# Moving the distances ahead of the update, and conv1 one place away from the first turn of x, in a 64-graph GNN kernel

## The chip, the cores and the metric

The kernel runs on one core of one Trainium2 chip. The metric is the device time of one execution in microseconds (us). Single executions of one kernel scatter by some us out of 2250 here, so differences of a few us are read from five rounds with a 95% interval, and from where instructions start in the traces.

## The reference

64 graphs of 256 nodes with 256 features pass two layers. Cut to what matters:

```python
# layer 0
xc = x^T;  h = relu(bn(conv1d(xc, conv1_w, 0)))           # conv1: one tap
h  = bn(conv1d(h, conv2_w, 8));  x_conv = relu(h + xc)^T   # conv2: 17 taps
s  = x @ w_se.T + b_se
A  = exp(-(|s_n|^2 + |s_m|^2 - 2 s_n.s_m)) * adj           # "distances", exp, mask
x_nmp = A @ relu(x @ w_msg.T + b_msg)                      # "messages", "passing"
r, z  = sigmoid(gates of [x_conv, x_nmp] and x)            # rz
n     = tanh(gi_n + r * gh_n)                              # the update's tanh
x = layernorm(x + (1-z)*n + z*x)                           # x1; h is its normalized form
# layer 1
h = layernorm(x)
x = layernorm(x + relu(adj @ h @ W_rel + b_rel + h @ W_root))   # project, aggregate, y
```

## The kernel before

The 64 graphs go through in 8 batches of 8. While the graphs of one batch pass through both layers, conv1 and conv2 of the next batch are dealt out between their steps. conv2 is turned into 16 small products per feature block ("filter products", `ps_k`), with trees of sums on VectorE around them. The order on every engine is the order in which the program issues; I call it the engine's queue. The trace shows it on ScalarE: in batch 1 the exp started at 288.72, behind a tanh that started at 288.19, though its distances were done near 287. `bank(...)` hands out one of the eight PSUM tiles of one pool (`bufs=8`), to which the matmuls here write; a new product on such a bank comes after the reading of the older one, and this shows as waits: in the profile of before the filter products stood 11.6 us, over 14 places, for the exp that reads the distances.

Two things make up the stream. The generator `conv(b)` hands out the convolution; each `yield None` ends a place:

```python
def conv(b):
    ...
    for g in range(0, BG, 2):                        # four pairs of graphs
        for c in range(C):                           # "turn" of x on TensorE
            ps = bank("ps_xTc")
            for j in range(4):
                nc.tensor.transpose(ps[:, j*P:(j+1)*P], xn[:, j, c*P:(c+1)*P], ident)
            nc.scalar.copy(xTc[:, c, :], ps)                          # L458
        nc.scalar.dma_start(out=xt_dram[pair], in_=xTc)
        fetch(g + 4)
        yield PE_WEIGHT
        yield None
        pss = []
        ...                                          # conv1: ps_c <- w1, xTc (L466), relu (L482)
    yield None
    if b > 0:
        yield from fold(0, BG)                       # DVE, 128x2048 each (L432)
    ...

def products(b, first, sums):                        # one triple of filter products
    p1, p2, p3 = bank("ps_k1"), bank("ps_k2"), bank("ps_k3")
    ...
    def take():
        nc.scalar.copy(k1, p1)                                        # L400
        nc.vector.tensor_sub(..., k1, p3)                             # L401
        nc.vector.tensor_add(..., k1, p2)                             # L402
    return take
```

The loop over the graphs interleaves it, one `pump()` at a time. `step(up)` runs the next part of the update, `step(y_left)` the last part of the graph before:

```python
def distances(k):                                    # ps_dist (L685), exp (L687)
    pss = [bank("ps_dist") for _ in range(C)]
    for m in range(C):
        nc.tensor.matmul(pss[m][:, :N], lr[r, 0, m*P:(m+1)*P], lr[r, 1, :], ...)
    for m in range(C):
        nc.scalar.activation(AT[k][:, m, :], pss[m][:, :N], AF.Exp, bias=ns[:, m:m+1], scale=2.0)

def update(k):
    stt(nn, ...); stt(nn, ...)                       # DVE (L104)
    nc.scalar.activation(nn, nn, AF.Tanh)            # L833
    yield                                            # first step ends
    nc.vector.tensor_sub(w, XG[k], nn)               # L837, then two more on w, then stats
    ...                                              # q, sh on GpSimd (L846 to L851)
    yield                                            # second step ends
    ...                                              # h on DVE (L856), x1 on ScalarE (L859)
    yield

def aggregate(k):
    ...                                              # ps_out, y on DVE, q and sh on GpSimd
    yield
    for n in range(C):
        nc.scalar.activation(y[:, n, :], ...)                         # L910
    nc.scalar.dma_start(out=out[k]..., in_=y)                         # L911
    yield

for k in ...:                                        # the graphs of batches 0 to 6
    up = update(k)
    gates_rz(k, 0);   pump()
    gates_n(k, 0);    step(y_left);   pump()
    transposes_h(k - 1);              pump()
    gates_rz(k, 1);   pump()
    passing(k + 1);   pump()
    factors(k + 2);   gates_n(k, 1);  pump()
    project(k - 1)
    step(up);         pump()
    distances(k + 2)
    step(up);         pump()
    messages(k + 3)
    step(up);         pump()
    mask(k + 2)
    agg = aggregate(k - 1); step(agg); step(agg); pump()
    y_left = agg
```

The last batch has a loop of its own, without convolution, in which VectorE makes sums for a cheaper form of the gates (`ps_a`, `ps_d`, ...; L786, L791).

## Time and profile before

| | before |
|---|---|
| time, median of 3 runs (range) | 2256.24 us (2254.48 to 2259.09) |
| TensorE (PE) busy | 2210.0 of 2252.8 us, 98% |
| VectorE (DVE) / ScalarE (ACT) / GpSimd (POOL) busy | 76% / 34% / 21% |
| PE's largest waits | exp of the distances (L687) 11.6 us; copy of turned x (L458) 7.1; filter take (L401) 4.7 |

PE is the bound, and nothing in the change shortens its work. So only its waits are of interest: who released it, how long, and what it ran into next. The lines themselves stand in the prediction.

### The profile page before, as it was taken

To read this page: it belongs to the slowest core of one execution; us is meant where nothing else is said; L and a number is where in the kernel's file an instruction comes from. 1 tells how busy PE (TensorE), PEld (TensorE's weight loads), DVE (VectorE), ACT (ScalarE), POOL (GpSimd) and SP (SyncE) were. 2 spreads that over 40 slices of the span, in tenths; PEclk is the share of its full clock that TensorE was granted. 3 is DMA by queue.
4 is the path that set the end of the run, shared out by engine and by line. 5 is a ranking of instruction groups with operands and counts; after the bars stand their busy time and mean duration, and the time that the engine had idled before them with its cause. 6 is when DMAs were issued, how large, how long until landed. Compare 5 with 4: busy or idle time off the path is not lost.

```text
span 2252.8 us, 24641 instructions
## 1 busy us (share of the span) xinstructions
PE 2210.0 (98%) x8400; PEld 1465.9 (65%) x8400; DVE 1721.0 (76%) x3329; ACT 767.1 (34%) x1587; POOL 469.8 (21%) x933
## 2 busy tenths in 40 slices
PE   8999999999999999999999999999999999999998
PEld 5775666666666666656766566665666666666665
DVE  6976889478892988749987498965979478896675
ACT  6433223432235322443224432244222432224333
POOL 0101212221221221203212221221212222212212
PEclk9999999999999999999999999999999999999999
DMA  5931432314423143232522334222432314321110
GB/s 148 317 111 60 143 108 84 103 52 140 135 76 103 38 151 120 75 107 67 167 72 76 102 114 142 76 87 74 131 122 75 113 52 140 114 85 50 42 33 20
DMA packets 212682, 226.69 MB, mean 101 GB/s; under 512 B 22103, under 2 KB 203854, under 8 KB 212558
## 3 DMA queue, kind: packets, MB, share of 16 engines
q1 hardware_dynamic: 190128, 191.27, 26.8%
q10 hardware_dynamic: 22430, 33.86, 4.3%
q8 instruction: 67, 1.10, 0.2%
q14 instruction: 57, 0.47, 0.1%
HBM read 179.22 MB, written 45.88 MB: 100 GB/s over the span
## 4 chain that ended last, share of the span: by engine, by line
PE 80%; DVE 15%; issue 2%; POOL 1%; ACT 1%; DMA 1%; ACTq 0%; SPq 0%; POOLq 0%; DVEq 0%
PE ps_rz L715 15%; PE ps_k L385 11%; PE ps_rz L713 8%; PE ps_n L727 7%; PE ps_out L882 7%; PE ps_c L466 5%; DVE XF L104 5%; PE ps_nmp L697 5%; PE ps_msg L647 4%; PE ps_out L894 4%; PE ps_n L725 4%; PE ps_w L230 2%; DVE w L104 2%; DVE bst L824 1%; PE ps_dist L685 1%
## 5 line engine op out<-in xcount | busy, mean ns | idle before, releaser
L104 DVE SCALAR_TENSOR_TENSOR XF<-XF 128x512 f32<-128x512 f32 (+2 forms) x800 | 507.8, 665 | 7.4
L846 POOL TENSOR_SCALAR q<-mv 128x2 f32<-128x2 f32 x63 | 31.9, 506 | 1442.1 <-DVE mv L825 1442.1
L385 PE MATMUL ps_k<-w,XF 128*128 128x256 f32 x1316 | 300.1, 384 | 12.9 <-ACT AT L687 11.6
L385 PEld LDWEIGHTS ps_k<-w,XF 128*128 128x128 f32 x1316 | 248.0, 191 | 59.8 <-ACT AT L687 17.3
L728 DVE TENSOR_TENSOR gn<-ps_n,brzn 128x512 f32<-128x512 f32 x114 | 78.4, 688 | 198.1 <-PE ps_n L727 198.1
L719 ACT ACTIVATE rz<-rz 128x512 f32<-128x512 f32 x114 | 71.8, 630 | 463.5 <-DVE rz L718 463.5
L882 PE MATMUL ps_out<-wrr,hT 128*128 128x512 f32 x504 | 226.6, 592 | 0.0
L713 PE MATMUL ps_rz<-whh,xT 128*128 128x512 f32 x456 | 215.6, 595 | 0.0
L715 PE MATMUL ps_rz<-wih,xc 128*128 128x512 f32 x456 | 214.3, 592 | 0.0
L715 PE MATMUL ps_rz<-wih,nmp 128*128 128x512 f32 x456 | 214.3, 592 | 0.0
L718 DVE TENSOR_TENSOR rz<-ps_rz,brzn 128x512 f32<-128x512 f32 x114 | 77.7, 682 | 152.9 <-PE ps_rz L715 152.9
L882 PEld LDWEIGHTS ps_out<-wrr,hT 128*128 128x128 f32 x504 | 95.9, 190 | 96.1 <-issue 84.6
L715 PEld LDWEIGHTS ps_rz<-wih,xc 128*128 128x128 f32 x456 | 86.7, 190 | 109.0 <-issue 108.8
L715 PEld LDWEIGHTS ps_rz<-wih,nmp 128*128 128x128 f32 x456 | 86.7, 190 | 109.0 <-issue 109.0
L658 ACT ACTIVATE msg<-msg 128x512 f32<-128x512 f32 x61 | 38.4, 630 | 339.2 <-DVE msg L656 339.2
L647 PE MATMUL ps_msg<-wms,xT 128*128 128x260 f32 x512 | 131.8, 395 | 4.7 <-DVE XF L401 4.7
L362 DVE TENSOR_TENSOR XF<-XF 128x512 f32<-128x512 f32 (+3 forms) x128 | 126.2, 1011 | 1.7
L466 PE MATMUL ps_c<-xTc,w 128*128 128x512 f32 x256 | 116.1, 596 | 7.1 <-ACT xTc L458 7.1
L697 PE MATMUL ps_nmp<-AT,msg 128*128 128x256 f32 x512 | 121.1, 379 | 0.0
L713 PEld LDWEIGHTS ps_rz<-whh,xT 128*128 128x128 f32 x456 | 82.8, 192 | 58.2 <-issue 55.0
L894 PE MATMUL ps_out<-hr,adj 128*128 128x256 f32 x504 | 119.6, 380 | 0.0
L883 ACT COPY hr<-ps_out 128x256 f32<-128x256 f32 x126 | 46.8, 372 | 213.8 <-PE ps_out L882 213.8
(197 smaller groups left out, 3790.2 us busy)
## 6 DMA issues: line engine op xcount, KB each, us to landing
w<-w2m SPq DMA_DIRECT2D x105, 768.0 KB, 5.9
xn<-in_x_dram SPq DMA_DIRECT2D x32, 512.0 KB, 4.4
xt<-xTc ACTq DMA_DIRECT2D x32, 512.0 KB, 3.3
xT<-xt SPq DMA_DIRECT2D x64, 256.0 KB, 3.0
xb<-in_x_dram SPq DMA_DIRECT2D x32, 512.0 KB, 5.9
adj<-in_adjT_dram SPq DMA_DIRECT2D x64, 256.0 KB, 2.8
x<-in_x_dram SPq DMA_DIRECT2D x64, 256.0 KB, 3.0
out_dram<-y ACTq DMA_DIRECT2D x63, 256.0 KB, 2.2
```

Source lines behind the costliest of these rows:

```text
L104: nc.vector.scalar_tensor_tensor(o, in0, s, in1, op0=op0, op1=op1)
L362: (nc.vector.tensor_add if add else nc.vector.tensor_sub)(sl(o, n), sl(a, n), sl(b, n))
L385: nc.tensor.matmul(ps, X[:, slot, c * P:(c + 1) * P], w(m, c), start=(c == 0), stop=(c == C - 1))
L466: nc.tensor.matmul(pss[o], w1[:, c, o * P:(o + 1) * P], xTc[:, c, :], start=(c == 0), stop=(c == C - 1))
L647: nc.tensor.matmul(ps[:, :D + 4], XT[k][:, c, m * P:(m + 1) * P], wms[:, c, :], start=(c == 0), stop=(c == C - 1 and not idle))
L697: nc.tensor.matmul(ps[:, d * N:(d + 1) * N], MSG[k][:, m, d * P:(d + 1) * P], AT[k][:, m, :], start=(m == 0), stop=(m == C - 1))
L713: nc.tensor.matmul(prz, XT[k][:, c, q], whh[:, c, 0:2 * D], start=(c == 0), stop=False)
L715: nc.tensor.matmul(prz, t, wih[:, i, 0:2 * D], start=False, stop=(i == 3))
L725: nc.tensor.matmul(pn[:, D:], XT[k][:, c, q], whh[:, c, 2 * D:], start=(c == 0), stop=(c == C - 1))
L727: nc.tensor.matmul(pn[:, :D], t, wih[:, i, 2 * D:], start=(i == 0), stop=(i == 3))
L882: nc.tensor.matmul(ps, hT[:, c, n * P:(n + 1) * P], wrr[:, c, :], start=(c == 0), stop=(c == C - 1))
L894: nc.tensor.matmul(po, ADJ[k][:, m, n * P:(n + 1) * P], hr[:, m, :], start=False, stop=(m == C - 1), skip_group_check=True)
```

## The change

Its intent is to remove the two largest waits of PE: the copy of turned x gets more time before conv1 reads it, and the exp of the distances no longer queues on ScalarE behind a tanh that is waiting for VectorE. The diff in full:

```diff
@@ conv(b) @@
             fetch(g + 4)
             yield PE_WEIGHT
             yield None
+            if b > 0 and g == 0:
+                yield None
             pss = []
@@ the loop over the graphs @@
             if k > 0:
                 project(k - 1)
+            if k + 2 < B:
+                distances(k + 2)
             step(up)
             pump()
-            if k + 2 < B:
-                distances(k + 2)
             step(up)
             pump()
@@ the loop of the last batch @@
         project(k - 1)
-        step(up)
         if k + 2 < B:
             distances(k + 2)
+        step(up)
         step(up)
```

I call the three hunks part 1 (place of conv1), part 2 (exp first, in the loop) and part 3 (exp first, in the last batch).

## The prediction

> **What bounds the kernel now.** I read first the busy shares of the page, then the waits of PE, then the timeline at the places where PE waits. The busy shares:
>
> ```profile
> span 2252.8 us, 24641 instructions
> ...
> PE 2210.0 (98%) x8400; PEld 1465.9 (65%) x8400; DVE 1721.0 (76%) x3329; ACT 767.1 (34%) x1587; POOL 469.8 (21%) x933
> ```
>
> The change alters no matmul, so only the 42.8 us that PE isn't busy can be won; some 8 us of them are start and end. The view of waits for PE names the rest:
>
> ```profile
> PE ps_k L385 <- ACT AT L687: 11.6, 14, 1.1
> PE ps_c L466 <- ACT xTc L458: 7.1, 10, 1.8
> PE ps_msg L647 <- DVE XF L401: 4.7, 13, 0.5
> PE ps_xc L574 <- DVE XF L104: 3.4, 1, 3.4
> PE ps_hT L869 <- DVE h L856: 2.6, 1, 2.6
> ...
> PE ps_a L786 <- DVE XF L791: 0.9, 1, 0.9
> ```
>
> (columns: total us, times, longest.) The change aims at the first two: the exp (L687) frees the PSUM bank that a product of the filters (ps_k) takes over, and the copy of the turned x (L458) is what conv1 (ps_c) reads. So the ceiling is about 19 us, 0.8%. But a wait counts only if PE isn't held a moment later by somebody else. The timeline (start, duration) at a wait of the first kind, from batch 1:
>
> ```profile
> 283.02 0.69 DVE L728 TENSOR_TENSOR gn<-ps_n,brzn 128x512 f32<-128x512 f32 x1 [4.17 <-PE ps_n L727]
> ...
> 286.35 0.70 PE L685 MATMUL ps_dist<-lr 4*128 4x256 f32 x4
> ...
> 288.19 0.63 ACT L833 ACTIVATE nn<-nn 128x512 f32<-128x512 f32 x1 [1.36 <-DVE nn L104]
> 288.72 0.82 ACT L687 ACTIVATE AT<-ps_dist,ns 128x256 f32<-128x256 f32 x2
> 289.23 4.58 PE L385 MATMUL ps_k<-w,XF 128*128 128x256 f32 x20 [1.12 <-ACT AT L687]
> ...
> 294.17 0.68 DVE L401 TENSOR_TENSOR XF<-XF,ps_k 128x512 f32<-128x512 f32 x1
> ...
> 294.91 1.14 PE L647 MATMUL ps_msg<-wms,xT 128*128 128x260 f32 x4 [0.22 <-DVE XF L401]
> ```
>
> The distances are ready at about 287, but the exp queues behind the tanh, which waits for DVE until 288.19. That is the wait meant. Yet 5.7 us later PE stands again, for L401 on DVE. From gn at 283.02 to L401 I followed every row of DVE: each starts where the one before ends, with no idle time. The start at 283.02 was set by PE before either wait.
>
> At a conv1, and in the last batch:
>
> ```profile
> 434.30 0.60 PE L869 MATMUL ps_hT<-ident,h 128*128 128x128 f32 x4
> 434.90 1.07 ACT L458 COPY xTc<-ps_xTc 128x512 f32<-128x512 f32 x2 [0.58 <-PE ps_hT L869]
> 435.54 3.70 PE L466 MATMUL ps_c<-xTc,w 128*128 128x512 f32 x8 [0.64 <-ACT xTc L458]
> ...
> 2154.94 0.53 DVE L791 TENSOR_TENSOR XF<-ps_a,brzn 128x384 f32<-128x384 f32 x1
> ...
> 2156.20 1.89 PE L786 MATMUL ps_a<-wsum,XF 128*128 128x256 f32 x6
> ```
>
> Only four small transposes lie between the turn of x and conv1. In the last batch PE writes onto the bank of ps_a 0.73 us after DVE has read it: little slack.
>
> [...]
> - [...] the exp ran 288.72, behind a tanh that came late, though its input was done near 287.
> - [...] So a tile takes the bank of an earlier one, and the order in which banks come free decides. The waits on L687 and L401 agree: both name readers of older tiles.
> - [...] swapping them reloads nothing. The trace agrees: one table load, 1283 ns, in the whole run.
> - [...] So I measure PE's losses from start to start.
>
> **Part 1, conv1 one place later (7 batches).** The order of instructions on PE changes here alone: the gates rz of the second half (12 records, 5.1 us) move between the first turn and conv1, and each later turn and conv1 slides by one, the last conv1 landing behind the distances. The copies need 1.07 us plus a hop, so the wait goes. Its size, start to start: from ps_hT at 434.30 to the next turn at 439.07 are 4.77 us; four transposes cost 0.43 and eight records of conv1 3.43 elsewhere, so 0.9 us are lost. Six batches look so: 6 x 0.9 = 5.4 us. The later conv1s get the neighbours that the next one has now (nmp, then sT and n), which show no wait; the last gets ps_out and dist, 4 us.
>
> Side effect on DVE: the folds now come after the update's w. In the first batch, graph 0, DVE stands 1.89 us before the folds, then w follows, and PE waits 2.64 us for h (transposes at 204.03). Now w fills that idle stretch. By hand: distances near 187.6, exp until 189.3, tanh until 189.9, w 190-193.2, folds (6.6 us) until 199.8, message sums until 200.8, h until 201.5. PE is ready near 200.7, so the transposes start near 201.5: 2.5 us won, with the 0.5 us of its conv1 inside. In the six other batches h is done near 474.6 against PE near 476: no wait either way.
> Part 1: 5.4 + 2.5 = 7.9 us.
>
> **Part 2, distances ahead of the update, in the filter products.** PE's order doesn't change, only ScalarE's: exp, exp, tanh. The exps end near 287.8, the bank is free when PE wants it (two products after 286.98, that is 287.84), and the wait on L687 goes: 7 x 1.12 and 7 x 0.54, all 11.6 us. But the second ps_msg of each still waits for L401; I checked in the built program that this dependence is the same. L401 ends at 294.85 whatever the exp does, as DVE runs without a gap from 283.02 and w, the only step that needs the tanh, starts at 290.14 by its place in DVE's queue, tanh or not. The second kind (332.08, gn at 326.45, L401 at 337.29) is the same. So PE reaches ps_msg sooner and stands there longer. Won: 0 us.
>
> **Part 3, the same swap in the last batch.** Here DVE waits for the tanh (w at 2169.81, after 0.69 us idle). An exp that waits for dist starts 0.80 us after it (118.16 to 118.96). So in a graph with dist at 2168.57: exps from 2169.37, tanh 0.74 us later at 2170.11 instead of 2169.15: w comes 0.96 us later, and DVE runs without a gap from there to L791. Slack at ps_a is 0.73 less 0.06 us of hop (L401's end to ps_msg's start above), 0.67 us; each of five graphs loses 0.3 us. The first has more slack (1.0 us), and loses 0.15. The last waits 0.92 us already and loses the full 0.95. With some 0.1 us for each new stop (conv1 took 3.70 after a wait, 3.60 without): 1.5 + 0.15 + 0.95 + 0.4 = 3.0 us lost. In the graphs before, w comes up to 1 us later too, but h has over 4 us of slack to its transposes there.
>
> **Sum.** 2256.2 - 7.9 - 0 + 3.0 = 2251.3 us.
>
> **The rivals.**
> - *Both waits really go.* Then part 2 gives 7 x 1.4 + 7 x 0.8 = 15 us start to start, and the time is near 2237. For it: it's the author's intent, and the largest wait in the view. Against it: the gapless DVE stretch and L401 behind each of these waits. I give it one in eight.
> - *Nothing moves.* The later tanh and the later fold cost what conv1 gives, by a wait for h or for a bank in the six conv stages: DVE there would have to be 1.4 us later than worked out. Then 2255 to 2258. One in five.
> - *ScalarE becomes late.* The exp at the head of its queue now holds tanh, and in the conv stages the relus of the last conv1 (folds). ACT is 34% busy, and its longest delay (tanh from 455.8 to 462) falls in time that DVE has to wait through anyway. If it hurt in every graph (0.5 us x 62), 2280. Under one in fifty.
>
> **Range and chances.** The steps err by some 2 us in part 1 and 2 us in part 3; the runs before spread over 4.6 us; the first rival pulls the low end. 2243 to 2257 holds 8 in 10. A 2% change is 45 us, more than all of PE's idle time, so faster by that is excluded short of a mistake (0.005), slower needs a new wait in every graph (0.01).
>
> **What would show each step.** Part 1: no wait of ps_c on L458 in batches 1 to 7 (what is left, 3.3 us, is batch 0), and ps_hT waiting under 1 us. Part 2: the wait on L687 gone, and the one of ps_msg on L401 grown from 4.7 to some 16 us; if it stays near 5 us, the step is wrong and the time falls by 10 us more. Part 3: ps_a on L791 grown from 0.9 us once to 3-4 us in 6 or 7. A wait of ps_hT or ps_rz in the conv stages, or of ps_k on DMA, would be one that I have missed.

## The result

| | runs | median (range), us | ratio to before, 95% |
|---|---|---|---|
| before | 4 | 2256.03 (2254.48 to 2259.09) | |
| after | 4 | 2246.36 (2244.61 to 2248.10) | 0.9955 [0.9938, 0.9973] |
| before, another chip session | 9 | 2255.19 (2254.00 to 2259.19) | |
| after, same session | 5 | 2247.50 (2244.39 to 2247.63) | 0.9959 [0.9946, 0.9971] |

A ratio is the mean time of one kernel's runs over that of the other's of the same rounds, so not quite the ratio of the medians. The change gains 0.4%, within the predicted range.

In the profile after, the page's first lines:

```profile
span 2246.3 us, 24617 instructions
...
PE 2202.2 (98%) x8400; PEld 1463.0 (65%) x8400; DVE 1721.5 (77%) x3329; ACT 769.2 (34%) x1587; POOL 511.7 (23%) x933
```

PE's waits (columns: us in total, times, longest; line numbers are 2 higher than before from L463 on):

```profile
PE ps_msg L649 <- DVE XF L401: 20.3, 14, 1.6
PE ps_xc L576 <- DVE XF L104: 3.4, 1, 3.4
PE ps_c L468 <- ACT xTc L458: 2.3, 3, 0.8
...
PE ps_a L788 <- DVE XF L793: 1.8, 1, 1.8
```

The wait on the exp has left the list, and so have the conv1 waits of batches 1 to 7. But the wait on L401 has gone from 4.7 to 20.3 us, over 14 graphs: the third wait of the list before has taken over all of the first. The same graph of batch 1 as in the prediction, in the timeline (start, duration):

```profile
278.79 0.69 DVE L730 TENSOR_TENSOR gn<-ps_n,brzn 128x512 f32<-128x512 f32 x1 [4.17 <-PE ps_n L729]
...
282.75 5.45 PE L385 MATMUL ps_k<-w,XF 128*128 128x256 f32 x24
282.85 0.84 ACT L689 ACTIVATE AT<-ps_dist,ns 128x256 f32<-128x256 f32 x2 [0.25 <-PE ps_dist L687]
283.96 0.63 ACT L835 ACTIVATE nn<-nn 128x512 f32<-128x512 f32 x1 [0.27 <-DVE nn L104]
...
289.94 0.68 DVE L401 TENSOR_TENSOR XF<-XF,ps_k 128x512 f32<-128x512 f32 x1
...
290.68 1.14 PE L649 MATMUL ps_msg<-wms,xT 128*128 128x260 f32 x4 [1.60 <-DVE XF L401]
```

The exp runs ahead of the tanh, without a new table load (ScalarE has one, 1283 ns, in the whole run, as before), and all 24 products run without a stop. Yet from gn to L401 are 289.94 - 278.79 = 11.15 us, and before they were 294.17 - 283.02 = 11.15 us: VectorE's queue did not move, and PE, early by the wait that it saved, stands 1.60 us for it instead of 0.22.

At the first conv1 of a batch:

```profile
430.18 1.10 ACT L912 ACTIVATE y<-y,sh,q 128x256 f32<-128x256 f32 x2 [0.43 <-POOL sh L909]
...
431.78 1.07 ACT L458 COPY xTc<-ps_xTc 128x512 f32<-128x512 f32 x2 [0.51 <-ACT y L912]
...
435.75 3.60 PE L468 MATMUL ps_c<-xTc,w 128*128 128x512 f32 x8
```

Twelve records of the gates (430.60 to 435.75, not shown) now lie between the transposes of h and conv1, and conv1 does not stop. In the last batch the exp pushes the tanh back, and the bank of ps_a comes late:

```profile
2161.64 0.84 ACT L689 ACTIVATE AT<-ps_dist,ns 128x256 f32<-128x256 f32 x2 [0.25 <-PE ps_dist L687]
2162.37 0.63 ACT L835 ACTIVATE nn<-nn 128x512 f32<-128x512 f32 x1
2163.03 0.69 DVE L839 TENSOR_TENSOR w<-x,nn 128x512 f32<-128x512 f32 x1 [1.56 <-ACT nn L835]
...
2172.06 0.52 DVE L793 TENSOR_TENSOR XF<-ps_a,brzn 128x384 f32<-128x384 f32 x1
...
2172.64 1.99 PE L788 MATMUL ps_a<-wsum,XF 128*128 128x256 f32 x6
```

With ps_dist at 2160.91, w starts 2.12 us after it; before it was 1.24 us (2168.57 to 2169.81). PE starts on the bank 0.58 us after VectorE began to read it, with no slack left; before it was 1.23 us (2178.87 to 2180.10).

Comparing the starts of the same PE instructions in the two traces gives where the time went: stretch of the first batch -5.3 us; the six later first conv1s -0.90, -0.83, -0.85, -0.86, -0.85, -0.85; the filter-product stretches together +0.4; the last batch +2.5 (0.16, five times 0.29, 0.86). Ahead of all of them the after trace is 1.1 us late, in the setup that the change does not touch.

### The profile page after: what moved, and what is told of

The parts are those of the page before. It is cut to its first block, busy times and chain, and to the rows that moved or that the text cites.

```text
span 2246.3 us, 24617 instructions
## 1 busy us (share of the span) xinstructions
PE 2202.2 (98%) x8400; PEld 1463.0 (65%) x8400; DVE 1721.5 (77%) x3329; ACT 769.2 (34%) x1587; POOL 511.7 (23%) x933
## 4 chain that ended last, share of the span: by engine, by line
PE 84%; DVE 12%; DMA 1%; issue 1%; POOL 1%; ACT 1%; SPq 0%; POOLq 0%; ACTq 0%; DVEq 0%
PE ps_rz L717 16%; PE ps_k L385 10%; PE ps_rz L715 8%; PE ps_n L729 8%; PE ps_out L884 7%; PE ps_c L468 5%; PE ps_nmp L699 5%; PE ps_msg L649 5%; PE ps_out L896 4%; PE ps_n L727 4%; DVE XF L104 4%; PE ps_w L230 2%; PE ps_dist L687 1%; DMA w<-w2m 1%; PE ps_hT L871 1%; DVE w L104 1%
## 5 line engine op out<-in xcount | busy, mean ns | idle before, releaser
L104 DVE SCALAR_TENSOR_TENSOR XF<-XF 128x512 f32<-128x512 f32 (+2 forms) x800 | 507.6, 665 | 7.4
L848 POOL TENSOR_SCALAR q<-mv 128x2 f32<-128x2 f32 x63 | 45.5, 723 | 1395.1 <-DVE mv L827 1395.1
L385 PE MATMUL ps_k<-w,XF 128*128 128x256 f32 x1316 | 294.2, 381 | 3.2 <-DMA w<-w2m 1.9
L649 PE MATMUL ps_msg<-wms,xT 128*128 128x260 f32 x512 | 131.4, 394 | 20.3 <-DVE XF L401 20.3
L649 PEld LDWEIGHTS ps_msg<-wms,xT 128*128 128x128 f32 x512 | 92.6, 189 | 54.7 <-DVE XF L401 26.0
```

The costliest lines, as they stand in the source:

```text
L104: nc.vector.scalar_tensor_tensor(o, in0, s, in1, op0=op0, op1=op1)
L385: nc.tensor.matmul(ps, X[:, slot, c * P:(c + 1) * P], w(m, c), start=(c == 0), stop=(c == C - 1))
L649: nc.tensor.matmul(ps[:, :D + 4], XT[k][:, c, m * P:(m + 1) * P], wms[:, c, :], start=(c == 0), stop=(c == C - 1 and not idle))
```

## The experiments

Twelve runs in three calls of four, each five rounds. All outputs are right. "Before" in each table is that of the same call.

### First call: the parts one at a time

Theory: part 1 gains what conv1 and the first batch waited; part 2 does nothing, as L401 takes the time back; part 3 costs. Rival: the parts' effects come from elsewhere, and the sum is right by accident.

**e1_place**: hunk 1 alone.

```diff
+            if b > 0 and g == 0:
+                yield None
```

> Only the extra place between the first turn of x and conv1; distances stay where they were. Theory (the whole gain is in this part): about -10 us in the trace, 6 x 0.86 us at the later conv1s and about 3.8 us in the first batch; the wait of ps_k on the exp stays at 11.6 us in 14 places, ps_c on xTc falls from 7.1 to some 2.3 to 3.3 us, ps_hT on h from 2.6 to about 0.5 us; no loss in the last batch. Time 2245 to 2248. Rival (the swap on ScalarE makes half of the gain): -5 us, 2251.

**e2_loop**: hunk 2 alone (the seven diff lines of the loop above).

> Only the swap in the loop of the first seven batches: nothing but ScalarE's order differs (exp ahead of tanh). Theory: the wait of ps_k on the exp goes from 11.6 us to 0, the wait of ps_msg on DVE L401 grows from 4.7 to about 20 us, and the time stays, 2255 to 2257 (0 +- 1 us). Rival (the removed wait is a gain): 10 to 15 us faster, 2241 to 2246.

**e3_tail**: hunk 3 alone.

> Only the swap in the loop of the last batch. Theory: it costs: tanh comes about 0.9 us later, w behind it, and PE waits for DVE at the second ps_a: some 0.16 + 5 x 0.29 + 0.86 = 2.5 us in the trace, 2258 to 2259. Rival (tanh has slack, as in the graphs before): 0 us.

**e4_place_loop**: hunks 1 and 2, the last batch as before.

> The change without its third hunk (the last batch as before). Theory: 2.5 us faster than the whole change, about 12 us faster than before, 2243 to 2245; ps_a waits 0.9 us as before, not 1.8. Rival (the last batch loses for another reason, such as its later start): like the whole change, 2246 to 2247.

| | median (range), us | ratio, 95% |
|---|---|---|
| before (11 runs) | 2254.43 (2251.07 to 2257.20) | |
| e1_place | 2247.81 (2245.64 to 2254.68) | 0.9975 [0.9961, 0.9988] |
| e2_loop | 2261.69 (2258.91 to 2262.98) | 1.0031 [1.0019, 1.0043] |
| e3_tail | 2257.68 (2257.39 to 2258.88) | 1.0015 [1.0003, 1.0027] |
| e4_place_loop | 2244.93 (2243.55 to 2246.73) | 0.9957 [0.9946, 0.9969] |

e1 and e4 came as expected, and e3 0.3 us below its range; e1's gain of 6.6 us is nearer to the 7.9 of the prediction than to the 10 that I expected of its trace. **e2 was a miss: alone, part 2 costs 7 us.** Its waits show the exchange that I expected (exp gone, L401 at 20.2 us) but also conv1's wait on the copy of turned x, at 12.9 us instead of 7.1. The starts of PE step back by exactly 1.0 us at each of the six later first conv1s, against the kernel before. The timeline of e2 there:

```profile
435.80 1.09 ACT L910 ACTIVATE y<-y,sh,q 128x256 f32<-128x256 f32 x2 [0.43 <-POOL sh L907]
...
437.40 1.07 ACT L458 COPY xTc<-ps_xTc 128x512 f32<-128x512 f32 x2 [0.51 <-ACT y L910]
...
438.04 3.70 PE L466 MATMUL ps_c<-xTc,w 128*128 128x512 f32 x8 [1.64 <-ACT xTc L458]
```

and of the kernel before (the copy at 434.90 and conv1 at 435.54 stand in the prediction):

```profile
433.22 1.09 ACT L910 ACTIVATE y<-y,sh,q 128x256 f32<-128x256 f32 x2 [0.43 <-POOL sh L907]
434.35 0.45 ACTq L911 DMA_DIRECT2D out_dram<-y  x1
```

The copy stands in ScalarE's queue behind the scaling of y and the issue of its store. The tanh is 1 us later, and with it w (after 3.23 us of idle VectorE instead of 2.15), h, y and, through the queue, the copy. The kernel before shows something else: there too the copy started only when y's store had been issued (434.35 + 0.45 = 434.80), although its input, the turn at 433.43, had been under way for long. So the wait that part 1 was made for may come from y's place in the queue, not from too few instructions on PE. That was tested in the third call.

### Second call: is it L401 that takes the gain back?

**after_again**: the changed kernel unaltered.

> The changed kernel once more, unaltered, as the yardstick of this chip and to see how far two profiles of one kernel differ. 2244 to 2249 us. TensorE's wait of ps_msg on the update of XF at L401 stays near 20 us over 14 places, the wait on AT stays gone. The theory that the larger part of the first batch's gain was chance (TensorE at a lower granted clock after its waits in the profile of before) expects no lower clock to be needed for a gain: the net of the first batch against a profile of before without the clock drop should be near -2.5 us.

**e5_after_swap**: the changed kernel, and in a graph whose pump holds filter products the pump comes ahead of the update's second step, so that L401 and L402 stand in VectorE's queue ahead of the w chain:

```diff
             step(up)
             pump()
+            filtering = STAGE.get(b + 1) == "products"
+            if filtering:
+                pump()
             step(up)
-            pump()
+            if not filtering:
+                pump()
```

> The changed kernel with one thing moved: in a graph of the filter-product stage, the pump whose take holds L401 and L402 comes ahead of the update's chain on w, so those two stand in VectorE's queue before the w chain. Theory (what the swap of exp and tanh took off the wait on AT was handed to the wait on L401, so the time hardly moved): the 20 us of ps_msg on L401 shrink to under 5 us, the wait on AT stays gone, and the run is 12 to 20 us below the changed kernel of the same rounds, 2227 to 2235 us. Rival (the product stages are set by VectorE or by the weight transfers, and the 1.3 to 1.6 us for each graph would come back at any next wait): within 3 us of the changed kernel, with a new wait of about the same size named in the list of waits, such as ps_k on a transfer or ps_out on hr.

**e6_before_swap**: the same edit on the kernel before.

> The kernel before with the same move of the pump alone, exp still behind tanh. Theory (AT is the later of the two waits there, and its 0.8 us for each graph stays): the 4.7 us of ps_msg on L401 go, the 11.6 us on AT stay, so 3 to 6 us below the kernel before, about 2250. Rival (moving the take is what gains, the swap of exp and tanh does not matter to it): as much as between the changed kernel and its own version with the move, 12 us or more below the kernel before.

**e7_e4_swap**: the same edit on e4_place_loop.

> The move of the pump on the version with the new place of conv1 and the swap in the loop, but the last batch as before: 2 to 3 us below the changed kernel with the move, as the last batch's swap costs 2.5 us: 2225 to 2232 us, the fastest of all. If the move brings nothing, 2244 to 2246.

| | median (range), us | ratio, 95% |
|---|---|---|
| before (9 runs) | 2255.19 (2254.00 to 2259.19) | |
| after_again | 2247.50 (2244.39 to 2247.63) | 0.9959 [0.9946, 0.9971] |
| e5_after_swap | 2224.69 (2224.57 to 2225.54) | 0.9864 [0.9849, 0.9879] |
| e6_before_swap | 2245.74 (2244.78 to 2249.60) | 0.9960 [0.9947, 0.9972] |
| e7_e4_swap | 2222.55 (2222.31 to 2222.78) | 0.9853 [0.9840, 0.9867] |

The theory holds, and the rival (VectorE or the weights would take it back once more) falls: e5 is 22.8 us below the changed kernel, a little more than expected. Neither the wait on the exp nor that on L401 is in its list. The same graph in e5:

```profile
278.31 0.69 DVE L730 TENSOR_TENSOR gn<-ps_n,brzn 128x512 f32<-128x512 f32 x1 [4.17 <-PE ps_n L729]
...
286.22 0.68 DVE L401 TENSOR_TENSOR XF<-XF,ps_k 128x512 f32<-128x512 f32 x1
287.55 1.92 PE L649 MATMUL ps_msg<-wms,xT 128*128 128x260 f32 x8
287.75 0.68 DVE L839 TENSOR_TENSOR w<-x,nn 128x512 f32<-128x512 f32 x1
```

L401 comes 7.91 us after gn instead of 11.15, the eight message products run in one go, and w, which is now behind, has slack: no wait on h appears in its place (ps_hT on h is 0.5 us once). e7, without part 3, is the fastest, 33 us (1.5%) below the kernel before.

e6 gained 9.5 us where I expected 3 to 6, though not the 12 of the rival. In its trace 2.2 us of this lie in the first batch, which the edit does not touch (next section), and 7.1 behind it, of which the list of before explains 4.7 (13 waits). I did not settle the remaining 2.4; a stop can cost more than the wait that is listed, as the prediction found 0.1 us with conv1 (3.70 us against 3.60), and 13 of these would be 1.3.

### Third call: what each is worth behind the other

**e9_loop_y**: e2_loop with the step of y moved from ahead of the copy of turned x to behind the transposes of h. No other engine's order differs from e2's.

```diff
-            step(y_left)
             pump()
             if k > 0:
                 transposes_h(k - 1)
+            step(y_left)
             pump()
```

> The second part of the change alone, as in e2_loop, with the step that issues the final scaling of y (and its store) moved behind the transposes of h, so that it stands behind the copy of the turned x in ScalarE's queue instead of ahead of it. Theory (alone, the second part costs some 6 us because y, made 1 us later by the later tanh, holds up the copy that conv1 waits for, at six conv1s): the wait of ps_c on xTc falls from 12.9 us back to about 7 us or less, and the run is 5 to 7 us below e2_loop, that is 2254 to 2257, like the kernel before. Rival (the 1 us at each conv1 comes from something else that the later tanh delays, such as h): the wait stays near 12.9 us and the run near 2261.

**e10_place_swap**: part 1 and the edit of e5, but the tanh ahead of the exp everywhere, as before. Against e7 this is the worth of part 2 when L401 is out of the way.

> Conv1 one place later and the move of the pump that takes L401 ahead of w, but the exp behind the tanh as before, everywhere. Against e7 (the same with the exp ahead of the tanh in the loop) this gives what the swap of exp and tanh is worth once L401 is out of its way. Theory: the wait on AT of 11.6 us (1.1 and 0.5 us in turn, 14 places) is back, and costs 11 to 16 us start to start: 2234 to 2239 us. Rival (the swap is worth nothing, the move of the pump does it all): within 3 us of e7, 2222 to 2226.

**e1_place_again**, **e4_place_loop_again**: unaltered.

> The first part alone once more, beside e4_place_loop_again, because their difference (2.9 us in the medians of the first call, over traces that drift by 1 to 2 us) does not settle whether the second part has a worth of its own on top of the first. 2246 to 2249 us.

> The first and second parts, the last batch as before. If the second part brings nothing, as predicted, within 1.5 us of e1_place_again; if it does bring something although the wait moved to L401, 2 to 4 us below it: 2243 to 2246.

| | median (range), us | ratio, 95% |
|---|---|---|
| before (23 runs) | 2256.23 (2251.54 to 2260.26) | |
| e9_loop_y (17 runs) | 2250.57 (2246.42 to 2253.80) | 0.9975 [0.9967, 0.9982] |
| e10_place_swap | 2241.11 (2239.15 to 2243.18) | 0.9932 [0.9920, 0.9944] |
| e1_place_again | 2247.40 (2242.67 to 2248.81) | 0.9957 [0.9946, 0.9969] |
| e4_place_loop_again | 2244.21 (2243.30 to 2246.40) | 0.9947 [0.9935, 0.9959] |

**e9** is 11 us below e2, which ran in the first call (by the ratios to each call's own before it is 13), so the rival (h or something else delays conv1) falls. I expected 5 to 7: the list shows conv1's wait at 3.2 us, 3.0 of it in batch 0, so not only e2's extra 1.0 us for each batch but the 0.9 us of the kernel before went too:

```profile
432.15 1.07 ACT L458 COPY xTc<-ps_xTc 128x512 f32<-128x512 f32 x2 [0.18 <-PE ps_xTc L457]
...
434.56 1.08 ACT L910 ACTIVATE y<-y,sh,q 128x256 f32<-128x256 f32 x2
...
432.82 3.67 PE L466 MATMUL ps_c<-xTc,w 128*128 128x512 f32 x8
```

The copy now starts 0.64 us after the turn (431.51), conv1 0.67 after the copy, without a stop, and at its old place. So y and its store in the queue were the cause of the wait (which of the two weighs more was not separated); part 1 removes it by giving PE something else to do meanwhile.

**e10 and e7** are apart by 18.6 us, or 17.8 by the ratios, as e7 ran in the second call. e10 came 2 us above what I expected. Here the swap of exp and tanh is worth its full size, and the move of L401 is worth much more behind it than without it. All four have part 1; medians in us, those of two calls where there are two:

| | L401 behind w | L401 ahead of w |
|---|---|---|
| tanh ahead of exp | 2247.81, 2247.40 (e1) | 2241.11 (e10) |
| exp ahead of tanh | 2244.93, 2244.21 (e4) | 2222.55 (e7) |

PE's starts in e7 against e10 step forward by 1.39 us in the first kind of graph and by 0.80 in the second, at nearly every one of the seven batches: the 1.4 and 0.8 us that the prediction gave its first rival, 15.4 us together. In e10's trace one graph shows a further 1.7. There, just behind the 1.12 us wait on the exp that ends at 1361.36, the granted clock is half for 3.41 us (columns: length, busy us of PE, weight loads, DVE, ACT, POOL, granted clock, DMA share, GB/s):

```profile
1358.06:1361.47 3.41, 2.29 (x11) 1.09 (x10) 3.34 (x6) 1.53 (x4) 0.00 (x0) 1.00 0.00 0
1361.47:1364.88 3.41, 3.41 (x9) 2.70 (x10) 3.38 (x8) 0.68 (x2) 0.00 (x0) 0.50 0.02 5
```

Half of 3.41 is those 1.7 us, and 17.1 of the difference have a place. e10's list has the wait back:

```profile
PE ps_k L385 <- ACT AT L689: 11.6, 14, 1.1
```

**e1 against e4**, twice: 2.9 and 3.2 us in the medians. So part 2 on top of part 1 gains some 3 us, not nothing. A good part of it is probably the granted clock, not the wait itself. Every run has its mean clock on record, and I take span x (1 - clock) as an estimate of the time lost to it: on average 7.9 and 5.6 us in e1's two sets of runs, 4.9 and 4.5 in e4's. So up to 2.9 and 1.1 us of the 3.8 and 2.3 by which the mean times differ go with the clock. The traces show where it falls. In the six with the 1.12 us waits on the exp (before, both of e1, e3, e6, e10) it is half for 3.41 us just behind 7 of these 42 waits, at least once in each trace. In the six where the swap has turned them into 1.6 us waits on L401 (after, its repeat, e2, both of e4, e9) it is so behind none of 42. No run tests this link alone, and about 1 us stays open: behind the first batch, e4's two traces take 1982.1 and 1982.0 us from the first filter product to the last matmul, e1's two 1983.8 (with two such stretches) and 1980.7 (with one).

## Why the prediction was right, and where not

The time was inside the range, 4.9 us below the middle. The prediction had no term for the clock: the loss, worked out as for e1 and e4, is 6.2 us on average over the 43 runs of before in the three calls and 3.0 over the nine of after, so up to 3.2 of the 9.7 us won are clock. Without them the gain would be some 6.5 us (an estimate), where the steps add up to 4.9. By its own steps:

**Part 1, -7.9 us: right, with the cause misnamed.** e1 gave -6.6 and -8.8 us in the medians. The six conv1s gave 5.1 us of the predicted 5.4. For the cause the step said that the copies need their 1.07 us plus a hop, and "only four small transposes lie between"; e9 shows that four transposes are enough when y isn't ahead in ScalarE's queue. The profile of before names PE (ps_hT, 434.30) as the releaser of that copy, after 0.58 us of idle ScalarE, and not the issue of y's store, which lasted until 434.80.

**The first batch, -2.5 us: right, once the clock is taken out.** The two traces differ by 5.3 us there. Since PE does the same work in every version, the start from the turned tiles (ps_xc) to the transposes of h can be laid side by side over all 14 traces, sorted by the granted clock of the window 142 to 153 us, just behind PE's 3.4 us wait for L104 (2.5 us in e10, whose stretch is the shorter for it):

| ps_xc to ps_hT, us | clock 0.69 in that window | clock 0.84 |
|---|---|---|
| conv1 at the old place | 72.33 (before), 72.44 (e2) | 71.32 (e3), 71.31 (e6), 71.25 (e9) |
| conv1 one place later | 69.82 (after_again), 69.91 (e1), 69.90 (e4) | 68.54 (after), 69.16 (e1 again), 68.58 (e4 again), 68.84 (e5), 68.91 (e7), 68.37 (e10) |

At equal clock the place is worth 2.1 to 3.0 us, as predicted; a lower clock costs 1.0, and falls on either kernel. Then there is a second such place that only the old order has: the 2.64 us wait for h. The windows 200 to 212 us (columns: length, busy us of PE, weight loads, DVE, ACT, POOL, granted clock, DMA share, GB/s) of before:

```profile
200.00:212.00 12.00, 9.36 (x27) 5.25 (x26) 10.90 (x19) 3.26 (x6) 6.07 (x10) 0.86 0.09 22
```

and of e6, with the same order on PE and the same wait:

```profile
200.00:212.00 12.00, 9.36 (x35) 5.55 (x34) 10.93 (x18) 3.26 (x6) 6.08 (x10) 1.00 0.04 15
```

The clock is 0.86 in two of the five traces that have this wait (before, e2) and 1.00 in the other three, and in all nine without it. So the wait costs 2.5 us or, where the clock falls with it, some 1 to 1.5 more (53.04 and 52.80 us from there to the next filter product, against 51.40 to 51.91). The prediction counted the wait alone; it missed this extra gain, which comes only in some executions.

**Part 2, 0 us: the mechanism is right, the number holds for no context exactly.** That L401 takes the wait over was predicted (16 us; 20.3 measured, which is 4.7 and the 15.4 start to start) and e5 shows it by taking L401 away. But the step that failed is the sentence "PE reaches ps_msg sooner and stands there longer. Won: 0": it looked at the products and left out the conv stages, where the same swap makes the tanh later. Alone it costs 7 us (e2), by y and the copy behind it; in the change, part 1 hides this, and some 3 us are won (e4 against e1), much of that probably by the clock. Those 3 us are the largest part of the miss of the middle.

**Part 3, +3.0 us: right, somewhat too large.** The trace shows 0.16 + 5 x 0.29 + 0.86 = 2.47 us. e3 cost 3.2 us in the medians, and e5 is 2.1 above e7. The term that was mis-sized is the 0.4 for new stops: the 0.3 of each graph, read start to start, had it inside. The sign that the step named, ps_a waiting for L791 3 to 4 us in 6 or 7 places, did not come: the list has 1.8 us once, and the stops of 0.29 us show in the starts of PE alone.

**The rivals.** "Both waits really go" (2237) did not happen in the change, and did in e7, through one more edit and by the amounts given (1.4 and 0.8). "Nothing moves" fell: its later fold and later tanh cost nothing in the first batch. In that place h had the least to spare: h started at 200.77 in the after trace, at about the time PE was ready (the transposes at 201.33), and that by GpSimd's small steps, which were slow there: in the after trace three of q (128x2 and 128x4 elements) took 2.19, 2.10 and 2.96 us beside VectorE's 128x2048 folds of 6.67 us for three; in the before trace, without the folds, 0.24, 0.19 and 1.04. No run tests whether it was the folds that slowed them. The first of the three in the after trace:

```profile
193.33 2.19 POOL L848 TENSOR_SCALAR q<-mv 128x2 f32<-128x2 f32 x1 [41.81 <-DVE mv L827]
```

## What to carry to other kernels

Before a wait is removed, look at the next wait of the same engine behind it and ask whether its releaser moves as well; here that engine, VectorE, ran without a gap for the 11.15 us from gn to L401, the time was handed on whole (a wait of 0.22 us became one of 1.60), and the two had to be removed together: 3 us and 6 us for either alone were 25 us for both. When the order on one queue changes, follow everything that stands behind the delayed instruction, also through other engines and back (tanh, w, h, y, copy of x), in every stage of the program and not only in the one the change is aimed at. And when a copy is late, look at what stands ahead of it in its own queue, a store's issue (0.45 us here) included, before giving the reader of the copy more to do. Before a difference of a few us between two traces is explained, lay their granted clocks side by side.
